# A hand-written order of 374 steps per two image pairs, exchanged for another order of the same steps

## The chip, the core and the metric

The kernel runs on one core of a Trainium2 chip. The metric is the device time of one execution in microseconds. Three runs of the kernel before gave 2715.25, 2713.97 and 2707.4 us, with a median of 2713.97 us. One further execution was profiled.

The engines are named as in the profile: PE is TensorE's matrix multiplier (PEld its weight loads), DVE is VectorE, ACT is ScalarE, POOL is GpSimd, and SP is the engine that issues every DMA of this kernel.

## The reference

The input is a batch of 128 images with 128 channels of 16 x 16 points. Layer 0 is a quantised convolution block. Layer 1 treats the 256 points of an image as a sequence of tokens, runs a selective state-space model (SSD, chunks of 64) over it forwards and backwards, and adds a mixture of 8 experts of which each token uses 2. Cut to what the change touches:

```python
t = _to_tokens(x)                                  # (128, 256, 128)
u = layernorm(t)
for dir in (fwd, bwd):                             # bwd sees the sequence reversed
    z, xbc, dt = split(u @ in_proj)
    xbc = silu(causal_conv(xbc, conv_w, 4 taps))   # -> xh (256), B (64), C (64)
    dt = softplus(dt + dt_bias)                    # exp, ln
    L = exp(segsum(dt * A))                        # exp, per head and chunk
    y = (C B^T * L) @ (xh * dt) + carried states + D * xh
    yg = y * silu(z)
    h += (yg * rsqrt(mean(yg * yg))) @ out_proj
t = t + h
p = softmax(layernorm(t) @ router_w); top 2, renormalised
out = t + sum over the 2 experts of p_e * (layernorm(t) @ expert_w[e])
```

## The kernel before

The program has two stages. The first (up to about 300 us) does the two convolutions and leaves each pair of images, transposed to tokens, in DRAM (`y_d`). The second stage is a loop over the 64 pairs, and the change is in its order alone.

The work of one pair is cut into generator functions, `part_a` to `part_t` (L691 to L1126). Each `yield` ends a step, and nearly every step puts the work of one engine into the program. `part_a` loads and normalises the tokens and transposes them (`u_ps`, L700). `part_c` is done once for two pairs: it makes the time steps `dt` and their logarithms, with one Exp (L738) and two Ln (L742 and L762) on ACT, and sends the parts through DRAM (`parts_d`) into the operands `rows` and `cols`. `part_x` projects one of three blocks of one direction (`x_ps`, L814), starts the convolution on ACT (L826) and finishes it by three DVE passes that read the bank in PSUM (L832). `part_bc`, `part_sx` and `part_z` apply Silu on ACT (L841, L851, L861). `part_s` makes the exponents of the decay matrix by a matmul (`sg`, L903 or L905) and applies Exp on ACT (L913). `part_g` makes C B^T (L888), `part_m` multiplies on DVE (L919, L924), `part_xt` transposes (L869), `part_y` multiplies (L938, L944), gates on DVE (L950) and POOL (L954) and squares on ACT (L957). `part_n` and `part_r` make the norm (L963, L971, L977, L979), `part_o` is the output projection (L998), `part_e` the router, `part_p` the product of gate and tokens on POOL (L1103), and `part_f` the experts (L1115). `part_t` has one step: it loads the table set of ACT that holds both Exp and Ln (L1125).

PSUM has three groups of banks in this stage, by `BANKS`: "x" with 2, "y" with 2 and "o" with 4. `x_ps`, `z_ps` and `sg` share the two "x" banks. A bank is free again when the last step that reads it is done: for `x_ps` the third DVE pass, for `z_ps` the Silu, for `sg` the Exp.

The order of all steps is written out by hand, in a table `T` (L1131 to L1196) with `PERIOD = 374`: for each step of an even and of an odd pair it gives a place, and pair `i` has its steps at `i // 2 * PERIOD` plus that place. The steps are sorted by this number and put into the program in that order, so that each engine's queue is in that order too:

```python
steps += [(i // 2 * PERIOD + t, len(steps) + n, stream) for n, t in enumerate(places[i % 2])]
steps.sort(key=lambda step: step[:2])
```

The number is a rank and not a time. Every two pairs bring 374 steps, so one period of the loop is 374 steps of several pairs in different stages, and a place says where in the period a step stands when it is taken modulo 374. There are 32 periods.

ACT holds one set of function tables at a time. Exp, Ln and Silu need a set that holds them. Where the set that is loaded lacks the next function, the program that is built has a table load ahead of that activation, under the activation's own line; in the profile it is `ACT_TABLE_LOAD`. The kernel's own load in `part_t` is one more.

Of the kernel before, what the change touches and what calls it, by code (L numbers as in the profile page):

```python
# [34 lines left out]
def kernel(ctx: ExitStack, tc: tile.TileContext, a: dict):  # L35
# [311 lines left out]
    with tc.tile_pool(name="w1p", bufs=1) as w1p:  # L347
# [15 lines left out]
        with tc.tile_pool(name="setup1", bufs=1) as setup, tc.tile_pool(  # L363
# [10 lines left out]
            for i in range(NP):  # L374
                t = res.tile([P, 2, NT], F32, name=f"xr{i}", tag=f"xr{i}")
# [38 lines left out]
            for c in range(4):  # L414
# [34 lines left out]
                n = cuts[c + 1] - cuts[c]  # L449
# [673 lines left out]
    def part_t(i):  # L1123
# [5 lines left out]

    PERIOD = 374  # L1130
    T = {  # L1131
        ('a',): [[145, 195, 294, 297, 323, 329], [338, 382, 482, 490, 514, 537]],
        ('c',): [
            [543, 573, 580, 590, 602, 607, 621, 627, 636, 638, 646, 647, 652, 657, 664, 666, 669, 696, 719,
             740, 765, 776, 790, 830, 835, 838, 929, 936, 968, 1102],
        ],
        ('x', 0, 0): [[735, 737, 748, 750, 753], [908, 920, 924, 926, 931]],
        ('x', 0, 2): [[755, 768, 769, 772, 775], [938, 946, 955, 957, 959]],
        ('x', 0, 1): [[786, 798, 804, 811, 814], [975, 982, 992, 1003, 1004]],
        ('x', 1, 2): [[821, 822, 832, 840, 846], [1022, 1034, 1039, 1041, 1049]],  # L1140
        ('x', 1, 0): [[839, 843, 853, 865, 866], [1044, 1056, 1057, 1059, 1061]],
        ('x', 1, 1): [[886, 894, 897, 900, 912], [1074, 1083, 1084, 1095, 1097]],
        ('z', 1, 0): [[898, 905], [1101, 1106]],
        ('bc',): [[928, 963], [1115, 1162]],
        ('sx', 0): [[901], [1098]],
        ('z', 0, 0): [[913, 925], [1116, 1118]],
        ('sx', 1): [[935], [1125]],
        ('z', 1, 1): [[934, 942], [1123, 1136]],
        ('z', 0, 1): [[945, 951], [1138, 1147]],
        ('g', 0): [[984], [1182]],  # L1150
        ('s', 0, 0, 0): [[958, 966], [1148, 1154]],
        ('t',): [[1344], [1203]],
        ('xt', 0, 0): [[993, 1006], [1169, 1180]],
        ('s', 0, 1, 0): [[969, 978], [1158, 1161]],
        ('s', 0, 0, 1): [[979, 987], [1168, 1173]],
        ('s', 0, 0, 2): [[989, 1000], [1183, 1184]],
        ('m', 0, 0): [[1011, 1016], [1200, 1201]],
        ('xt', 1, 0): [[974, 997], [1155, 1159]],
        ('s', 0, 1, 1): [[1007, 1014], [1190, 1194]],
        ('s', 1, 1, 0): [[1015, 1018], [1202, 1208]],  # L1160
        ('s', 0, 1, 2): [[1023, 1035], [1249, 1252]],
        ('xt', 0, 1): [[1008, 1032], [1163, 1192]],
        ('s', 1, 0, 2): [[1051, 1060], [1258, 1266]],
        ('g', 1): [[1069], [1248]],
        ('m', 0, 1): [[1078, 1080], [1256, 1259]],
        ('s', 1, 0, 0): [[1062, 1065], [1241, 1250]],
        ('s', 1, 1, 1): [[1082, 1091], [1232, 1234]],
        ('xt', 1, 1): [[1090, 1094], [1280, 1295]],
        ('s', 1, 0, 1): [[1064, 1066], [1251, 1254]],
        ('m', 1, 1): [[1110, 1120], [1261, 1264]],  # L1170
        ('s', 1, 1, 2): [[1073, 1075], [1235, 1242]],
        ('y', 0, 1): [[1099, 1105, 1113, 1134], [1276, 1290, 1296, 1322]],
        ('y', 0, 0): [[1096, 1100, 1104, 1126], [1265, 1277, 1281, 1315]],
        ('m', 1, 0): [[1081, 1107], [1292, 1293]],
        ('y', 1, 1): [[1121, 1128, 1176, 1181], [1297, 1307, 1347, 1351]],
        ('y', 1, 0): [[1144, 1174, 1179, 1187], [1324, 1341, 1364, 1370]],
        ('n', 0): [[1157], [1360]],
        ('n', 1): [[1199], [1376]],
        ('r',): [[1205, 1216, 1218, 1222, 1231], [1391, 1401, 1402, 1410, 1421]],
        ('o', 0): [[1233, 1247], [1404, 1426]],  # L1180
        ('o', 1): [[1219, 1246], [1424, 1441]],
        ('e',): [
            [1255, 1273, 1284, 1288, 1301, 1304, 1311, 1313, 1318, 1323, 1326, 1327, 1330, 1335, 1336, 1339,
             1354, 1357, 1368, 1372, 1373, 1383, 1387, 1393, 1398, 1399, 1403, 1407, 1411, 1420, 1453],
            [1442, 1459, 1462, 1482, 1486, 1491, 1506, 1511, 1514, 1515, 1519, 1525, 1527, 1539, 1540, 1541,
             1544, 1549, 1551, 1565, 1567, 1585, 1589, 1595, 1597, 1598, 1599, 1600, 1602, 1603, 1610],
        ],
        ('p', 0): [[1466, 1509, 1545], [1643, 1652, 1680]],
        ('p', 1): [[1463, 1493, 1571], [1644, 1719, 1720]],
        ('f',): [  # L1190
            [1505, 1530, 1560, 1563, 1572, 1581, 1617, 1627, 1631, 1637, 1736],
            [1663, 1688, 1708, 1733, 1753, 1802, 1806, 1811, 1824, 1835, 1881],
        ],
        ('p', 2): [[1477, 1526, 1611], [1657, 1739, 1801]],
        ('p', 3): [[1584, 1618, 1619], [1796, 1803, 1820]],
    }  # L1196
    parts = {
        "a": part_a, "c": part_c, "x": part_x, "bc": part_bc, "sx": part_sx, "z": part_z, "xt": part_xt, "g": part_g,
# [45 lines left out]
```

## Time and profile before

| what | value |
|---|---|
| runs | 2707.4, 2713.97, 2715.25 us |
| profiled execution: time | 2710.16 us |
| profiled execution: span from first to last instruction | 2708.4 us |
| busy share of the span | PE 93%, DVE 89%, ACT 79%, POOL 61% |
| granted TensorE clock, mean | 0.984 |
| time from one start of L778 to the next in the loop | 72.47 to 72.49 us from the fourth period on |
| ACT table loads in the profile | L913 66, L851 64, L1125 64; 1283 ns each |

The span is 1.8 us shorter than the execution's own time. The loop's `r_ps` matmuls (L774, L778), which come once in a period, run from 326 us to 2551 us. The period repeats to within 0.02 us, so one period of it stands for all but the first three and the last.

### The profile page before, as it was taken

The numbers are of one execution on the slowest core, as the hardware profiler recorded it, in microseconds if no ns is written. First come the engines' busy times: TensorE is split into PE (matmuls) and PEld (weight loads), VectorE is DVE, ScalarE is ACT, GpSimd is POOL, SyncE is SP. The second block draws the span as 40 slices with busy tenths as digits, with TensorE's granted clock in tenths as the row PEclk, the third lists the DMA queues.
The fourth block names the chain that finished last, engine by engine and source line by source line (L and its number), as shares of the span: only waits on it lengthen the run. The fifth ranks groups of instructions, "written<-read, shape, count | busy, mean of one in ns | idle before, by whom it ended". The sixth has DMA issues, their size and how long they took to land.

```text
span 2708.4 us, 47861 instructions
## 1 busy us (share of the span) xinstructions
PE 2528.8 (93%) x16004; PEld 1486.2 (55%) x16004; DVE 2405.0 (89%) x6161; ACT 2129.3 (79%) x3750; POOL 1656.0 (61%) x1728
## 2 busy tenths in 40 slices
PE   0889589999999999999999999999999999999997
PEld 0335245565565555566555565555555566555553
DVE  8876579999999999999999999999999999999884
ACT  6877488888888888888888888888888888888872
POOL 1885315666666666666666666666666666666566
PEclk9999789999999999999999999999999999999998
DMA  8468211223322233322322223222223322322223
GB/s 273 157 219 273 102 29 57 92 88 96 95 92 83 76 95 96 95 88 87 96 82 79 92 89 94 96 92 89 72 93 95 96 88 89 93 88 76 85 84 110
DMA packets 165707, 275.59 MB, mean 102 GB/s; under 512 B 46528, under 2 KB 89536, under 8 KB 165440
## 3 DMA queue, kind: packets, MB, share of 16 engines
q1 hardware_dynamic: 165440, 272.32, 32.0%
q8 instruction: 132, 2.16, 0.3%
q14 instruction: 135, 1.11, 0.1%
HBM read 197.45 MB, written 58.03 MB: 94 GB/s over the span
## 4 chain that ended last, share of the span: by engine, by line
PE 69%; DVE 16%; ACT 7%; DMA 3%; issue 3%; POOL 1%; SPq 0%; POOLq 0%; DVEq 0%; ACTq 0%
PE f_ps L1115 11%; PE x_ps L814 9%; PE o_ps L998 8%; PE y_ps L938 8%; PE z_ps L857 7%; PE cv L221 4%; PE y_ps L944 4%; PE sg L903 3%; PE g_ps L888 3%; PE xt_ps L869 2%; DVE bc L832 2%; ACT e L913 2%; DVE xc L832 2%; PE sg L905 2%; DMA xr<-in_x 2%
## 5 line engine op out<-in xcount | busy, mean ns | idle before, releaser
L1103 POOL TENSOR_TENSOR gb<-gb,u2T 128x512 f32<-128x512 f32 x512 | 643.3, 1278 | 48.8 <-DMA gb<-gd 44.3
L832 DVE SCALAR_TENSOR_TENSOR xc<-x_ps,cw,xc 128x510 f32<-128x510 f32 (+2 forms) x768 | 571.3, 744 | 76.4 <-ACT xc L826 58.7
L913 ACT ACTIVATE e<-sg 128x512 f32<-128x512 f32 x768 | 449.4, 594 | 213.2 <-PE sg L903 172.5
L954 POOL TENSOR_TENSOR yg<-yg,z 128x512 f32<-128x512 f32 x256 | 326.0, 1279 | 432.7 <-DVE yg L950 430.7
L1115 PE MATMUL f_ps<-gb,ew 128*128 128x512 f32 x1024 | 519.0, 606 | 7.1 <-POOL gb L1103 6.9
L814 PE MATMUL x_ps<-uT,wx 128*128 128x512 f32 x768 | 406.5, 611 | 15.6 <-ACT e L913 5.8
L938 PE MATMUL y_ps<-e,xt 128*64 128x256 f32 x2048 | 319.3, 390 | 0.6 <-DVE e L919 0.6
L919 DVE TENSOR_TENSOR e<-e,g_ps 128x1024 f32<-128x1024 f32 x256 | 310.4, 1212 | 1.9 <-PE g_ps L888 1.9
L832 DVE SCALAR_TENSOR_TENSOR bc<-x_ps,cw,bc 128x510 f32<-128x510 f32 (+2 forms) x384 | 284.3, 740 | 10.6 <-ACT bc L826 8.1
L857 PE MATMUL z_ps<-uT,wz 128*128 128x512 f32 x512 | 275.8, 621 | 0.2
L998 PEld LDWEIGHTS o_ps<-wo,yg 128*128 128x128 f32 x2048 | 246.1, 193 | 25.3 <-issue 16.7
L998 PE MATMUL o_ps<-wo,yg 128*128 128x128 f32 x2048 | 251.5, 276 | 0.0
L826 ACT ACTIVATE xc<-x_ps,cb,cw 128x512 f32<-128x512 f32 x256 | 199.2, 778 | 63.0 <-PE x_ps L814 62.7
L1115 PEld LDWEIGHTS f_ps<-gb,ew 128*128 128x128 f32 x1024 | 171.1, 192 | 115.6 <-issue 93.7
L950 DVE SCALAR_TENSOR_TENSOR yg<-xc,dcol,y_ps 128x512 f32<-128x512 f32 x256 | 187.3, 742 | 53.0 <-PE y_ps L944 53.0
L963 POOL TENSOR_TENSOR sq<-sq,sq 128x512 f32<-128x512 f32 x128 | 163.1, 1274 | 113.5 <-ACT sq L957 113.5
L944 PE MATMUL y_ps<-e,xt 128*64 128x128 f32 x2048 | 198.9, 273 | 0.0
L903 PE MATMUL sg<-rows,cols 128*128 128x256 bf16 x1024 | 191.9, 274 | 7.5 <-DVE bc L832 2.3
L221 PE MATMUL cv<-hpad,wq 128*128 128x512 bf16 x640 | 179.4, 424 | 16.4 <-DVE hpad L194 8.6
L944 PEld LDWEIGHTS y_ps<-e,xt 128*64 128x64 f32 x2048 | 147.0, 137 | 74.1 <-DVE e L924 0.3
L861 ACT ACTIVATE z<-z_ps 128x512 f32<-128x512 f32 x256 | 152.3, 595 | 40.2 <-PE z_ps L857 38.4
L903 PEld LDWEIGHTS <-cols 128*128 128x128 bf16 x1024 | 91.8, 100 | 156.7 <-issue 143.8
(258 smaller groups left out, 5010.1 us busy)
## 6 DMA issues: line engine op xcount, KB each, us to landing
gb<-gd SPq DMA_DIRECT2D x256, 512.0 KB
xr<-in_x SPq DMA_DIRECT2D x64, 256.0 KB
y<-yt SPq DMA_DIRECT2D x64, 256.0 KB
yt<-y SPq DMA_DIRECT2D x64, 256.0 KB
cc<-bc SPq DMA_DIRECT2D x128, 128.0 KB
out<-ob SPq DMA_DIRECT2D x64, 256.0 KB
o<-o SPq DMA_DIRECT2D x59, 256.0 KB
q<-o SPq DMA_DIRECT2D x59, 256.0 KB
```

The source lines that it names most:

```text
L814: nc.tensor.matmul(ps, wx[d][:, n * P : (n + 1) * P], uTs[i], start=True, stop=True)
L832: nc.vector.scalar_tensor_tensor(acc[:, :, to], raw[:, :, of], cw[:, d, n, 3 - back : 4 - back], acc[:, :, to], ALU.mult, ALU.add,)
L857: nc.tensor.matmul(ps, wz[:, d, n * P : (n + 1) * P], uTs[i], start=True, stop=True)
L903: nc.tensor.matmul(sg[:, :, of], c_[:, k, d, s, half, :], r_[:, :, d, t, of], start=True, stop=True)
L913: nc.scalar.activation(e0[:, :, t, :] if j < 2 else e1, sg, AF.Exp)
L919: nc.vector.tensor_tensor(e0.rearrange("p h t l -> p h (t l)"), e0.rearrange("p h t l -> p h (t l)"), gps[i, d, k][:, 0:NT].unsqueeze(1).t ...
L938: nc.tensor.matmul(y_ps[64 * q : 64 * q + 64, k, :], xt[:, 2 * k + s0, 64 * h : 64 * h + 64], e0[:, h].rearrange("p t l -> p (t l)"), star ...
L944: nc.tensor.matmul(y_ps[64 * q : 64 * q + 64, k, s1 * P : (s1 + 1) * P], xt[:, 2 * k + s1, 64 * h : 64 * h + 64], e1[:, h, :], start=False ...
L954: nc.gpsimd.tensor_tensor(yg, yg, zs[i, d][:, n, :], ALU.mult)
L998: nc.tensor.matmul(o_ps[:, (2 * j + d) * P : (2 * j + d + 1) * P], ygs[i, d, n][:, t * P : (t + 1) * P], wo[d][:, n, :], start=(n == 0), s ...
L1103: nc.gpsimd.tensor_tensor(gb[:, e], gb[:, e], u2Ts[i], ALU.mult)
L1115: nc.tensor.matmul(f_ps, ew[:, e, :], gbs[i, e], start=False, stop=(e == NE - 1))
```

## The change

The diff changes only the places in `T`. All 374 steps of a period, their instructions, tiles and buffers, `PERIOD` and the numbers of banks stay. Its author describes it as the same steps in a fourth order, searched with measured waits between engines and with half a microsecond kept between DVE's passes over SBUF and POOL's products. The pipeline is as deep as it was: from the first `x` step of an even pair to the last `f` step of the odd one there are 1146 ranks in both tables (735 to 1881 before, 665 to 1811 after).

The lines of the diff that the text below speaks of:

```diff
-        ('c',): [
-            [543, 573, 580, 590, 602, 607, 621, 627, 636, 638, 646, 647, 652, 657, 664, 666, 669, 696, 719,
-             740, 765, 776, 790, 830, 835, 838, 929, 936, 968, 1102],
+        ('c',): [
+            [484, 494, 507, 518, 531, 552, 560, 573, 576, 579, 600, 606, 613, 620, 649, 651, 652, 659, 661,
+             671, 691, 698, 709, 726, 730, 756, 778, 789, 891, 1002],
...
-        ('x', 1, 2): [[821, 822, 832, 840, 846], [1022, 1034, 1039, 1041, 1049]],
-        ('x', 1, 0): [[839, 843, 853, 865, 866], [1044, 1056, 1057, 1059, 1061]],
+        ('x', 1, 2): [[754, 759, 768, 780, 792], [938, 949, 952, 956, 963]],
+        ('x', 1, 0): [[775, 779, 794, 796, 801], [964, 973, 978, 983, 986]],
...
-        ('t',): [[1344], [1203]],
-        ('xt', 0, 0): [[993, 1006], [1169, 1180]],
-        ('s', 0, 0, 1): [[979, 987], [1168, 1173]],
-        ('s', 0, 0, 2): [[989, 1000], [1183, 1184]],
+        ('t',): [[591], [1118]],
+        ('xt', 0, 0): [[914, 922], [1087, 1120]],
+        ('s', 0, 0, 1): [[913, 918], [1098, 1108]],
+        ('s', 0, 0, 2): [[921, 927], [1109, 1127]],
...
-        ('s', 0, 1, 1): [[1007, 1014], [1190, 1194]],
-        ('s', 1, 1, 0): [[1015, 1018], [1202, 1208]],
-        ('xt', 0, 1): [[1008, 1032], [1163, 1192]],
+        ('s', 0, 1, 1): [[937, 945], [1123, 1132]],
+        ('s', 1, 1, 0): [[946, 957], [1139, 1147]],
+        ('xt', 0, 1): [[940, 962], [1093, 1131]],
...
-        ('y', 0, 0): [[1096, 1100, 1104, 1126], [1265, 1277, 1281, 1315]],
-        ('y', 1, 1): [[1121, 1128, 1176, 1181], [1297, 1307, 1347, 1351]],
-        ('y', 1, 0): [[1144, 1174, 1179, 1187], [1324, 1341, 1364, 1370]],
-        ('r',): [[1205, 1216, 1218, 1222, 1231], [1391, 1401, 1402, 1410, 1421]],
+        ('y', 0, 0): [[1029, 1034, 1037, 1111], [1213, 1218, 1226, 1275]],
+        ('y', 1, 1): [[1057, 1069, 1113, 1119], [1239, 1247, 1260, 1299]],
+        ('y', 1, 0): [[1075, 1103, 1114, 1124], [1257, 1284, 1303, 1306]],
+        ('r',): [[1140, 1151, 1155, 1158, 1164], [1328, 1341, 1343, 1345, 1356]],
...
-            [1663, 1688, 1708, 1733, 1753, 1802, 1806, 1811, 1824, 1835, 1881],
+            [1622, 1645, 1668, 1672, 1676, 1696, 1716, 1743, 1763, 1766, 1811],
```

The order of a step's numbers is the order of its yields. In `c` the sixth is the Exp (L738), the eighth the first Ln (L742) and the eighteenth the second (L762). In `x` they are the matmul, ACT's start of the convolution and the three DVE passes; in `s` the matmul and the Exp; in `r` the matmul (`n_ps`, L971), ACT's copy (L977), the transpose (L979) and two small steps.

## The prediction

> **What bounds the kernel now.** I read the busy shares first, then the table of one period, then who waited for whom, then the timelines of PE and ACT at those waits.
>
> ```profile
> PE 2528.8 (93%) x16004; PEld 1486.2 (55%) x16004; DVE 2405.0 (89%) x6161; ACT 2129.3 (79%) x3750; POOL 1656.0 (61%) x1728
> 1174.70:1247.20 72.50, 71.61 (x474) 43.12 (x473) 67.65 (x176) 59.54 (x105) 46.13 (x46) 1.00 0.28 89
> ```
>
> The second line is one period (us: length, then busy PE, PEld, DVE, ACT, POOL, then clock). PE has 0.9 us of idle in 72.5, DVE 4.8, ACT 13.0. The period is set by PE's queue: its matmuls plus its waits. Busy time hides part of a wait, since a matmul's end is modelled, so I took PE from start to start. A 128x512 fp32 product (x, z, f; two passes) takes 0.86 us, a 128x512 `sg` 0.22, four transposes 0.44, `o` 1.79, `y` 1.45, `g` 0.86, `n` 0.57. All 103 groups of a period follow such fixed values, except three, which wait: 0.90, 0.26 and 0.24 us, together 1.39. The largest, ACT's timeline and then PE's:
>
> ```profile
> 1145.77 1.28 ACT L913 ACT_TABLE_LOAD   x1
> 1147.08 0.60 ACT L913 ACTIVATE e<-sg 128x512 f32<-128x512 f32 x1
> 1147.70 1.28 ACT L1125 ACT_TABLE_LOAD   x1
> 1148.99 0.63 ACT L957 ACTIVATE sq<-yg 128x512 f32<-128x512 f32 x1
> 1149.53 0.58 ACT L913 ACTIVATE e<-sg 128x512 f32<-128x512 f32 x1
> ...
> 1148.40 1.02 PE L814 MATMUL x_ps<-uT,wx 128*128 128x512 f32 x2
> 1150.16 0.38 PE L905 MATMUL sg<-rows,cols 128*128 128x512 bf16 x1 [0.73 <-ACT e L913]
> ```
>
> The `sg` at 1150.16 could have started 0.86 us after 1148.40. It needs the "x" bank that the Exp ending at 1150.11 reads, and this Exp stands behind two table loads and a square. The 0.24 us wait is of the same kind:
>
> ```profile
> 1191.34 1.28 ACT L1125 ACT_TABLE_LOAD   x1
> 1192.64 0.60 ACT L913 ACTIVATE e<-sg 128x512 f32<-128x512 f32 x1
> ...
> 1192.09 1.12 PE L1115 MATMUL f_ps<-gb,ew 128*128 128x512 f32 x2
> 1193.29 1.12 PE L814 MATMUL x_ps<-uT,wx 128*128 128x512 f32 x2
> ```
>
> The third, 0.26 us at 1184.21, waits for the last DVE pass of an `x_ps`, late because a small product before it (`sel`, L1055, otherwise 0.19 us) took 1.13 us beside one of POOL's. So table loads on ACT, not ACT's sum, make most of PE's wait, because only two banks lie between them and PE.
>
> **The change, part by part.**
>
> *What stays.* Every instruction of PE, DVE, POOL and SP, and the depth of the pipeline. Fill and drain I leave at nothing: their ranks are nearly the same. 31 periods carry the change.
>
> *PE's own work.* After a full 128x128 product, a run that uses part of the array (`y`, `g`, `n`, `dt`, `rt`) starts 0.094 us later, and a full product behind it costs 0.01 (`sg`), 0.06 (transposes) or 0.10 us (128x512) more: above, `f` and `x` have 1.12 where they otherwise have 1.02. There are 13 such runs in a period before and 15 after: 2 x 0.094 = 0.19; behind them 0.92 becomes 0.95; a pair of `y` that stood together is split, 0.15. Sum **+0.37 us**.
>
> *DVE beside POOL.* DVE's rows above their usual time (`sel` L1055 and L1058, `e` L1071, up to 1.28 for 0.15) come to about 4.3 us a period. Spacing can take these away. They are 4.3 us of DVE's time, but PE's path holds only the 0.26.
>
> *The removed waits.* I count all three as gone: **-1.39**. That is the most the change can gain on PE's path.
>
> *Table loads.* This is what a change of order brings with it. Before, modulo 374, `t` of the even pair stands at 222, ahead of the Exp (233) and the two Ln (253, 322) of `c`: its set serves all three. After, Exp is at 178, the first Ln at 199, `t` only at 217. The built program's ACT order shows the result: 32 loads at the first Ln (2 before) and 95 at L913 (66 before); the Silu phases still have 64. Per period 8 loads, not 6: 2 x 1.28 = 2.57 us of ACT, against 13.0 idle. What counts is where they stand. ACT after: Exp(0,1,1), **load**, Ln, x(1,2), **load**, Exp(1,1,0), xt, **load** (`t`), ns. PE: sg(0,1,1), x(1,2), xt, sg(1,1,0), f, n, x(1,0), f, nT. x(1,0) takes the bank that Exp(1,1,0) frees. These are the rows for ACT:
>
> ```profile
> L913 ACT ACTIVATE e<-sg 128x512 f32<-128x512 f32 x768 | 449.4, 594 | 213.2 <-PE sg L903 172.5
> L826 ACT ACTIVATE xc<-x_ps,cb,cw 128x512 f32<-128x512 f32 x256 | 199.2, 778 | 63.0 <-PE x_ps L814 62.7
> L742 ACT ACTIVATE lw<-w 128x64 f32<-128x64 f32 x32 | 8.0, 249 | 0.0
> L913 ACT ACT_TABLE_LOAD x66 | 84.7, 1283 | 1.2
> ```
>
> From the start of sg(0,1,1): matmul and hand-over 0.42, Exp 0.59, load 1.28, Ln 0.25, x 0.78, load 1.28, Exp 0.59, hand-over 0.1: x(1,0) at 5.3. PE has 0.22 + 0.86 + 0.44 + 0.22 + 0.95 + 0.57 = 3.26 us of work until then: **2.0 us of wait**. Without the two loads the sum is 2.7 and there is none. The first load can't run earlier: it is queued behind an Exp that waits for this very matmul. Then nT needs ns: Exp's end at 5.25 + xt 0.58 + load 1.28 + ns 0.27 + 0.05 = 7.4; PE is there at 5.3 + 0.96 + 0.86 = 7.1: 0.3 more. If ACT comes late to Exp(0,1,1) (squares, an xt and `c`'s Exp stand ahead), up to 0.8 is added. I take **2.7**, ends 2.0 and 3.1.
>
> *The odd pair's `t`* stands at 370, between Exp(0,0,1) and Exp(0,0,2) with three squares and an xt. From the first Exp's end: 3 x 0.63 + 1.28 + 0.58 + 0.59 = 4.4 us until x(1,2) gets its bank; PE has sg 0.31, g 0.86, f 0.96, sg 0.22 = 2.35, and more if it reaches sg(0,0,2) late, which its two f (1.7 us) suggest. Ends 0 and 2.0; **1.2**. The nearest row, the load at 1191.34, cost 0.24. The loads at the turns to Silu and from Silu to Exp stand beside `y`, `u2` and `z` work of over 2 us; I cost them at nothing, and at 1.28 each if ACT is behind there.
>
> *Clock.* A long wait can also slow what follows. At the loop's start the trace has:
>
> ```profile
> 398.70 1.98 PE L814 MATMUL x_ps<-uT,wx 128*128 128x512 f32 x2 [1.85 <-ACT e L913]
> 400.69 2.69 PE L998 MATMUL o_ps<-wo,yg 128*128 128x128 f32 x16
> ...
> 398.80:402.20 3.40, 3.40 (x11) 2.26 (x12) 1.25 (x3) 0.80 (x2) 1.01 (x1) 0.50 0.28 63
> ```
>
> After 1.85 us of idle the granted clock was 0.50 for 3.4 us, a loss of 1.7; after 1.30 us (at 427) it stayed at 1.00. A wait of 2.0 to 2.7 in each period may or may not do this; I take half of 1.7, **0.85**, ends 0 and 1.7.
>
> *The sum.* 0.37 - 1.39 + 2.7 + 1.2 + 0.85 = **+3.73 us** a period, x 31 = 116 us. On the profiled execution (2710.2; span 2708.4) that is 2826; the median of the runs lies 3.8 higher, so 2830.
>
> **Two rules weighed.** The Trainium skill, "ScalarE: Activation LUTs", section on what a table load costs, adds a drain to each load, 2.66 us per switch. Here the load at 1145.77 takes 1.28 and the Exp follows 0.03 later; by the page's figure the two loads would make the wait 2.8 us longer, an estimate of 85 us more in all. The row decides. The Trainium skill, "TensorE: Matmul & The Clock Gate", Part 1, has the clock fall after an idle window of about 3.4 us, so a wait of 2.7 would leave it alone and the sum would be 26 us less. The row at 398.70 shows a fall after 1.85 us of idle, so the half stays in.
>
> **The rivals.**
> *Faster: the loads hide.* With no wait on PE left, the period falls by 1.02: 31 x 1.02 = 32 us, 2682. For it: 13.0 us of ACT idle per period, and 4.3 us that DVE can win back. It decides once Exp(1,1,0) ends within 3.2 us of sg(0,1,1)'s start. Against it: matmul, two Exp, Ln, x and two loads in one queue are 5.2.
> *Only the sure part.* Waits of 2.0 and nothing else: +0.98 a period, 30 us, 2744.
> *Worse.* Both places at their ends and the clock falling at both: 3.1 + 2.0 + 3.4 - 1.02 = 7.5, 231 us, 2945; half-way to it from my sum is 2887.
> *The spacing isn't there.* Delayed squares and Exps shift POOL and DVE against each other, and DVE's stalls return; PE, waiting elsewhere, then loses 0.26 more at most, 8 us.
> *No change:* the loads cost about the 1.0 that the rest gains.
>
> **How the numbers follow.** My sum 0.62, only the sure part 0.16, worse 0.12, faster 0.07, no change 0.03. The range goes from just under the sure part, 2740, to 2895, a little over half-way to the worst; outside lie the faster and unchanged cases and part of the worse one. A measurement of this kernel tells about 0.3% (8 us) from no change: faster 0.07, same 0.03, slower 0.90.
>
> **What would show it.** Right: table loads of 1.28 us at L742, about 255 loads at L742, L861, L913 and L1125 together; PE's longest waits at x_ps after an Exp (L913), 2 us or more, once a period; r_ps starts some 76 us apart; ACT busier by 2.6 us a period. The clock step shows as 0.5 in some stretches inside the loop. Wrong: periods of 71.5 us, or PE waits that end at DVE or POOL, or fill and drain that grow.

## The result and the profile after

The changed kernel takes 2792.11 us (median of 4 runs, 2786.04 to 2795.79), the kernel before 2712.38 us (4 runs). The ratio is 1.0294, with a 95% interval from 1.0269 to 1.0318: slower by 80 us.

All of it lies in the loop. In the profiled executions it was 2223.6 us from the first of the 32 starts of L778 to the last, and is 2304.9 us, 81.4 more; what lies ahead of them is 1.1 us longer and what follows 1.2 us shorter. The page's first part, and the table of two neighbouring periods of the loop and of one stretch inside the second (us: length, busy PE, PEld, DVE, ACT, POOL, then the granted clock):

```profile
PE 2561.8 (92%) x16004; PEld 1496.3 (54%) x16004; DVE 2386.0 (86%) x6161; ACT 2205.4 (79%) x3808; POOL 1658.5 (59%) x1728
1207.80:1282.30 74.50, 72.12 (x473) 43.16 (x473) 66.96 (x176) 62.23 (x107) 46.21 (x45) 1.00 0.29 87
1282.30:1358.20 75.90, 73.60 (x473) 44.07 (x473) 67.08 (x176) 62.16 (x107) 46.19 (x45) 0.98 0.27 86
1338.10:1341.50 3.40, 3.40 (x8) 1.62 (x7) 0.89 (x6) 2.24 (x4) 0.08 (x1) 0.53 0.00 0
```

There are two kinds of period now: 74.50 us, and 75.9 us where the granted clock falls to half for 3.4 us. In 27 settled periods there are 12 of the second kind. ACT has 2.7 us more to do in a period than before (62.2 for 59.5), with 58 more instructions in the whole program. All of them are table loads (the groups of ACT, by line):

```profile
L913 ACT ACT_TABLE_LOAD x95 | 121.9, 1283 | 1.7
L1125 ACT ACT_TABLE_LOAD x64 | 82.1, 1283 | 1.1
L861 ACT ACT_TABLE_LOAD x64 | 82.1, 1283 | 1.1
L742 ACT ACT_TABLE_LOAD x32 | 41.1, 1283 | 0.6
```

This is where PE waits. ACT's timeline of the stretch with the first Ln, and PE's below it:

```profile
1258.40 0.60 ACT L913 ACTIVATE e<-sg 128x512 f32<-128x512 f32 x1 [0.21 <-PE sg L905]
1259.01 1.28 ACT L742 ACT_TABLE_LOAD   x1
1260.31 0.26 ACT L742 ACTIVATE lw<-w 128x64 f32<-128x64 f32 x1
1260.47 0.76 ACT L826 ACTIVATE bc<-x_ps,cb,cw 128x512 f32<-128x512 f32 x1
1261.25 1.28 ACT L913 ACT_TABLE_LOAD   x1
1262.54 0.60 ACT L913 ACTIVATE e<-sg 128x512 f32<-128x512 f32 x1
1263.04 0.58 ACT L873 COPY xt<-xt_ps 128x512 f32<-128x512 f32 x1
1263.63 1.28 ACT L1125 ACT_TABLE_LOAD   x1
1264.93 0.28 ACT L977 ACTIVATE ns<-n_ps 128x128 f32<-128x128 f32 x1
...
1263.19 1.13 PE L814 MATMUL x_ps<-uT,wx 128*128 128x512 f32 x2 [1.88 <-ACT e L913]
1264.15 1.02 PE L1115 MATMUL f_ps<-gb,ew 128*128 128x512 f32 x2
1265.26 0.33 PE L979 MATMUL n_ps<-ident,ns 128*128 128x128 f32 x1
```

The Exp that starts at 1262.54 frees the bank for the `x_ps` at 1263.19, and the copy at 1264.93 makes the `ns` that the transpose at 1265.26 reads. Three loads stand in six microseconds, in the order that the prediction has. The 1.88 us in the bracket are idle time. From start to start, as the prediction reckons, the wait of `x_ps` is 1.95 us: the `n_ps` ahead of it starts at 1260.67 and takes 0.57. The transpose waits 0.24 us, since the `f_ps` ahead of it takes 0.86.

Where the clock falls, the same place looks like this one period later:

```profile
1337.69 1.53 PE L814 MATMUL x_ps<-uT,wx 128*128 128x512 f32 x2 [1.88 <-ACT e L913]
1339.01 1.91 PE L1115 MATMUL f_ps<-gb,ew 128*128 128x512 f32 x2
```

The wait is the same 1.88 us, but `x_ps` takes 1.53 for 1.13 and `f_ps` 1.91 for 1.02.

### The profile page after: what moved, and what is told of

Its sections match the earlier page's. It is cut to its first block, busy times and chain, and to the rows that moved or that the text cites. A ratio compares the mean times of both kernels' runs of the same rounds, so it can differ in the third digit from the quotient of the medians.

```text
span 2789.7 us, 47812 instructions
## 1 busy us (share of the span) xinstructions
PE 2561.8 (92%) x16004; PEld 1496.3 (54%) x16004; DVE 2386.0 (86%) x6161; ACT 2205.4 (79%) x3808; POOL 1658.5 (59%) x1728
## 4 chain that ended last, share of the span: by engine, by line
PE 76%; ACT 15%; DVE 5%; issue 1%; DMA 1%; POOL 1%; SPq 0%; DVEq 0%; POOLq 0%; ACTq 0%
PE f_ps L1115 12%; PE x_ps L814 11%; PE y_ps L938 9%; PE z_ps L857 8%; PE o_ps L998 8%; PE cv L221 4%; PE sg L903 4%; PE y_ps L944 4%; PE xt_ps L869 3%; PE g_ps L888 3%; ACT e L913 3%; ACT L1125 2%; ACT sq L957 2%; PE sg L905 2%; ACT L913 2%
## 5 line engine op out<-in xcount | busy, mean ns | idle before, releaser
L1115 PE MATMUL f_ps<-gb,ew 128*128 128x512 f32 x1024 | 532.8, 614 | 8.0 <-POOL gb L1103 7.7
L814 PE MATMUL x_ps<-uT,wx 128*128 128x512 f32 x768 | 417.8, 627 | 75.5 <-ACT e L913 68.4
L986 POOL TENSOR_TENSOR rr<-rr,mhalf 128x8 f32<-128x8 f32 x64 | 106.6, 1666 | 175.9 <-DVE rr L982 175.9
L814 PEld LDWEIGHTS x_ps<-uT,wx 128*128 128x128 f32 x768 | 125.0, 194 | 135.0 <-ACT e L913 86.3
```

Of the source, the lines that this page charges most:

```text
L814: nc.tensor.matmul(ps, wx[d][:, n * P : (n + 1) * P], uTs[i], start=True, stop=True)
L1115: nc.tensor.matmul(f_ps, ew[:, e, :], gbs[i, e], start=False, stop=(e == NE - 1))
```

## The experiments

Theory L says that the table loads make PE's waits, by where they stand between two Exps. Rival O says that the rest of the new order makes them and that the loads fit into ACT's idle time. As `t` (L1125) is a step of its own that no other step waits for, it can be moved alone. A place with a half is a rank between two others. Each ratio is to runs of the kernel before on the same chip. The periods are from start to start of L778 in each run's trace.

**e1: the order after, `t` ahead of the first Exp of each pair.**

```diff
-        ('t',): [[591], [1118]],
+        ('t',): [[888.5], [1084.5]],
```

> The order after, with only the step t moved: ahead of the first Exp (L913) of each pair, at 888.5 and 1084.5. 4 table loads a period instead of 8. Theory L (the table loads make TensorE's waits): the waits of 1.95 us (x_ps behind an Exp), 0.24 (transpose of ns) and 0.39 us (x_ps of the odd pair) go, the granted clock stays at 1.00 in the loop, the period falls from a mean of 75.07 us to 71.5 to 71.9, and the time to about 2689 us (2683 to 2695), below both kernels. Rival O (the rest of the order makes the waits, and the loads fit into ScalarE's idle time): at least 2760 us.

Measured: 2681.95 us, ratio to before 0.9891 (0.9874 to 0.9907). The period is 71.77 to 71.80 us, and the granted clock stays at 1.00 through the settled loop. PE's wait for the Exp and the wait for `ns` are gone; so is the wait of `x_ps` in the odd pair. The wait of 0.37 us behind a DVE pass stays and is 0.39. Only the place of `t` differs from the changed kernel, and 110 us are gone. That settles L against O. (The time lies 1 us below the range that was expected.)

**e2: the order before, with the same move.**

```diff
-        ('t',): [[1344], [1203]],
+        ('t',): [[965.5], [1153.5]],
```

> The order before, with only the step t moved ahead of the first Exp (L913) of each pair, at 965.5 and 1153.5. 4 table loads a period instead of 6. Theory L: the waits of 0.90 and 0.24 us go, the 0.26 us behind a DVE pass stays; period 72.48 - 1.14 = 71.34 us, time about 2677 us. Rival O: 2712 us as before, within 5.

Measured: 2665.43 us, ratio 0.9831 (0.9815 to 0.9848), period 71.18 us. Two of the three waits of before are gone and the third is left. One line makes the kernel before faster by 1.7%. The period of e1 lies 0.6 us above it: 0.24 us is PE's own work, and the rest is waits, 0.15 more behind the DVE pass and 0.22 at `r_ps` (L774). So with the loads well placed in both, the new order is still the slower one, by 17 us.

**e3: the order after, only the even pair's `t` moved.**

```diff
-        ('t',): [[591], [1118]],
+        ('t',): [[888.5], [1118]],
```

> The order after, with only the even pair's t moved, to 888.5; the odd one stays at 1118. 5 loads a period, none left in the stretch with the first Ln. Theory L: the waits of 1.95 and 0.24 us and the half clock go, those of the odd pair (0.39 and 0.37) stay: period 72.3 us, time about 2706 us. Rival O: within 10 us of 2792.

Measured: 2696.34 us, ratio 0.9946 (0.9930 to 0.9963), period 72.24 to 72.26 us (expected 72.3), clock at 1.00. The waits of 0.39 and 0.37 us of the odd pair are as they were. The periods of e1 to e3 came within 0.2 us of what was expected, but the times came out 7 to 12 us lower. Part of that lies in the first three periods, in which the loop fills: they take 186.9, 185.7 and 190.2 us together, for 194.6 before the change and 202.9 after it.

**e4: the order after, only the odd pair's `t` moved.**

```diff
-        ('t',): [[591], [1118]],
+        ('t',): [[591], [1084.5]],
```

> The order after, with only the odd pair's t moved, to 1084.5; the even one stays at 591. 7 loads a period; the three loads in the stretch with the first Ln stay. Theory L: TensorE's wait of 0.39 us (x_ps of the odd pair, behind the load at t) goes, that of 0.37 us (sg behind a DVE pass) stays, and the waits of 1.95 and 0.24 us and the half clock stay: about 13 us less than 2792, 2780 (2765 to 2790). Rival: the odd pair's t matters as much as the even one's, half of the 110 us between e1 and the order after: 2737.

Measured: 2784.14 us, ratio 1.0283 (1.0266 to 1.0300). The wait of 0.39 us is gone and the periods without a half clock fall from 74.50 to 74.04 us, as L has it. But 20 of 27 periods now have the half clock (75.4 us), for 12 before, and that gives most of the gain back: 8 x 1.38 / 27 = 0.41 us a period for 0.46 won. The mean of the settled periods is 75.06 us, for 75.12 in the changed kernel, and most of the 8 us of difference in time lies in the first three periods (195.5 us for 202.9). The rival's 2737 is far off.

**e5: the order before, made to load as the order after does.**

```diff
-        ('t',): [[1344], [1203]],
+        ('t',): [[1400.5], [1203]],
```

> The order before, with only the even pair's t moved to 1400.5, behind the first Ln and two more Exps, as it stands in the order after. 8 loads a period; the stretch becomes Exp, load, Ln, xt, load, Exp, Exp, load, ns. Theory L: x_ps waits about 2.4 us and the transpose of ns about 1.0 us there, the wait of 0.90 us goes; 2.5 us more a period, and a half clock in part of the periods; about 2800 us (2770 to 2833). Rival O: 2712 us, within 10.

Measured: 2785.63 us, ratio 1.0279 (1.0262 to 1.0297), most periods 75.15 to 75.36 us. Moving one load costs the old order nearly all of what the whole change cost. ACT's stretch and PE's:

```profile
1326.13 1.28 ACT L742 ACT_TABLE_LOAD   x1
1327.43 0.26 ACT L742 ACTIVATE lw<-w 128x64 f32<-128x64 f32 x1
1327.59 0.57 ACT L873 COPY xt<-xt_ps 128x512 f32<-128x512 f32 x1
1328.18 1.28 ACT L913 ACT_TABLE_LOAD   x1
1329.47 1.08 ACT L913 ACTIVATE e<-sg 128x512 f32<-128x512 f32 x2
...
1328.30 0.64 PE L971 MATMUL n_ps<-sq,chosen 128*32 128x128 f32 x16 [0.65 <-POOL rstda L681]
1330.12 1.96 PE L814 MATMUL x_ps<-uT,wx 128*128 128x512 f32 x2 [1.18 <-ACT e L913]
```

Part of the wait I had put at `x_ps` shows at `n_ps` ahead of it (0.7 us from start to start; `x_ps` 1.2), 2.0 in all for the 2.4 expected. The transpose of `ns` waits 0.9 us in a period without a half clock, for the 1.0 expected. The profile's releaser for `n_ps` names POOL's `rstda`, which no matmul there reads; what `n_ps` waited for was not settled. The wait of 0.90 us behind the old place of the even `t` is gone.

**e6: the order after, the even pair's `t` directly ahead of the first Ln.**

```diff
-        ('t',): [[591], [1118]],
+        ('t',): [[572.5], [1118]],
```

> The order after, with the even pair's t moved to 572.5, directly ahead of the first Ln: 6 loads a period, as before the change, and one load instead of three between the Exp of sg(0,1,1) and ns. Theory L: the wait of x_ps falls by one load, from 1.95 to about 0.67 us, that of the transpose of ns goes, and with an idle time below 1 us the granted clock stays at 1.00: period 72.9 us, time about 2724 us (2710 to 2740). Rival (the number of loads counts, not their place): the kernel before has 6 loads too, so 2712.

Measured: 2715.6 us (7 runs), ratio 1.0029 (1.0017 to 1.0040), period 72.78 us (expected 72.9), clock at 1.00. One load in the stretch leaves a wait of 0.53 us at `x_ps`. With none (e3) it is 0, with two and a third for `ns` it is 1.95 and 0.24. The time alone lies between the two theories' numbers and nearer the rival's 2712; the traces tell them apart, since the waits that stay are 0.53, 0.39 and 0.37, other ones than the 0.90, 0.26 and 0.24 of before.

**e7 and e8: two costs that are left in e2, one each.** In e7 the odd pair's `y(0,1)` matmul stands directly behind `y(0,0)`, one run of part-array products fewer. In e8 the odd pair's first `sel` (L1055) stands behind the last DVE pass of `x(0,2)`.

```diff
 e7 (on e2), ('y', 0, 1), odd pair
-[1276, 1290, 1296, 1322]
+[1265.5, 1290, 1296, 1322]
 e8 (on e2), ('e',), odd pair
-[1442, 1459, 1462, 1482, 1486, 1491, 1506, 1511, 1514, 1515, 1519, 1525,
+[1442, 1459, 1462, 1482, 1486, 1491, 1506, 1511, 1514, 1515, 1523.5, 1525,
```

> The kernel of e2, with one PE step moved: the odd pair's y(0,1) matmul from 1276 to 1265.5, directly behind y(0,0) and ahead of z(1,0), so that one run of part-array products fewer stands in the period (12 for 13). If a run costs what the rows of before show (0.094 ahead of it, 0.15 for the split pair, 0.06 behind), the period falls by 0.30 us to 70.88 and the time by 9 us to about 2656. If y(0,1) then waits for DVE's products instead: 71.18 us, 2665, with the wait at y_ps.

> The kernel of e2, with one DVE step moved: the odd pair's first sel (L1055) from 1519 to 1523.5, behind the last DVE pass of x(0,2) instead of between its passes. This sel takes 1.13 us instead of 0.19 when it starts beside a product of POOL, and TensorE's last wait (0.24 us, sg) is for that last pass. Theory: the wait goes, the period falls to 70.94 us and the time by 7 us to about 2658. Rival (the stall moves to another step that TensorE waits for): 71.18 us or more, 2665.

Measured: e7 2654.65 us, ratio 0.9805 (0.9787 to 0.9823), period 70.88 us; e8 2656.48 us, ratio 0.9808 (0.9792 to 0.9825), period 70.95 us. Both periods are what the rows gave (70.88 and 70.94). DVE's timeline at the place, first of e2, then of e8:

```profile
1233.52 0.74 DVE L832 SCALAR_TENSOR_TENSOR bc<-x_ps,cw,bc 128x510 f32<-128x510 f32 x1
1234.17 1.13 DVE L1055 TENSOR_TENSOR sel<-lg,mx 128x32 f32<-128x32 f32 x1
1235.23 1.51 DVE L832 SCALAR_TENSOR_TENSOR bc<-x_ps,cw,bc 128x508 f32<-128x508 f32 x2
```

```profile
1226.35 2.30 DVE L832 SCALAR_TENSOR_TENSOR bc<-x_ps,cw,bc 128x510 f32<-128x510 f32 x3
1228.57 0.18 DVE L1055 TENSOR_TENSOR sel<-lg,mx 128x32 f32<-128x32 f32 x1
```

The three passes are now in one piece, and `sel` takes 0.18 us for 1.13.

**e9: e2, e7 and e8 together.**

> The kernel of e2 with the moves of e7 (y pair) and e8 (sel) together. Theory: the two gains add, since one is TensorE's own work and the other its last wait: period 71.18 - 0.30 - 0.24 = 70.64 us, time about 2647 us. Rival (without waits TensorE now catches up with ScalarE or VectorE, and a new wait takes their place): 2652 to 2657, no better than e7 or e8 alone.

Measured: 2649.69 us, ratio 0.9776 (0.9760 to 0.9792), period 70.64 us. It is the fastest version, 1.2% below e1 and 5.1% below the changed kernel. The theory's sum holds for the period to 0.01 us. PE has no wait of over 0.1 us left in the period: the 70.64 us are its matmuls.

## Why the prediction was right, point by point

The direction, the mechanism and the place were right, and the time lay inside the range (2740 to 2895), 38 us below the 2830 that was forecast. The sum per period was +3.73 us. Measured, a period without a half clock is 74.50 - 72.48 = 2.02 us longer, and 12 half clocks in 27 periods at 1.4 add 0.62: 2.64, times 31 is 82 us. Most terms were put too high.

*PE's own work, forecast +0.37.* Without the waits and the small delays that go with them the periods of the two orders are 71.18 and 70.94 us: +0.24. The price of a run of part-array products is right (e7, exact to 0.01 us); counting the rows of two orders by hand left an error of 0.13. One row was misread: the prediction explains the 1.12 us of the `x_ps` at 1193.29 by such a run, but a full product (`f_ps`) stands ahead of it. It has its extra 0.10 us behind the wait, and in e2, without the wait, that is gone.

*The removed waits, -1.39.* All three are gone, as counted; with that 0.10 us, and 0.06 us at an `xt_ps` that is gone in e2 too, they were 1.54.

*The stretch with Ln, forecast 2.7.* Measured 1.95 at `x_ps` and 0.24 at the transpose, 2.2. The chain from sg(0,1,1) to x(1,0) was put at 5.3 us and takes 5.2 (1257.98 to 1263.19). What failed is the allowance on top of the minimum of 2.0 + 0.3: ACT was not late at the first Exp. The bracket in its row says so, it waited 0.21 us for PE.

*The odd pair's `t`, forecast 1.2.* This term was too large: x(1,2) waits 0.39 us. ACT, PE and DVE at the place:

```profile
1294.09 1.28 ACT L1125 ACT_TABLE_LOAD   x1
1295.38 0.63 ACT L957 ACTIVATE sq<-yg 128x512 f32<-128x512 f32 x1
1295.92 0.57 ACT L873 COPY xt<-xt_ps 128x512 f32<-128x512 f32 x1
...
1296.95 0.39 PE L905 MATMUL sg<-rows,cols 128*128 128x512 bf16 x1 [0.21 <-DVE xc L832]
1297.55 1.13 PE L814 MATMUL x_ps<-uT,wx 128*128 128x512 f32 x2 [0.21 <-ACT e L913]
...
1294.31 1.15 DVE L1055 TENSOR_TENSOR sel<-lg,mx 128x32 f32<-128x32 f32 x1
```

Two things were missed. Neighbouring activations overlap by about 0.1 us (the copy starts at 1295.92, the square ends at 1296.01), so the chain is 4.0 us and not 4.4. And PE comes to it later, because it waits 0.37 us just before, at `sg`, for a DVE pass; with it the place costs 0.8.

*DVE beside POOL.* The change is described as keeping DVE's passes over SBUF away from POOL's products. The stalls did not go away, they moved: in each period three rows of DVE are 0.7 to 1.1 us above their usual time, all beside a product of POOL (L1055 twice and L1065), 2.8 us together; before there were four (L678, L1055, L1058, L1071), 3.4 us. DVE's busy time in a period falls from 67.65 to 66.96. One of the three, the `sel` at 1294.31 above, takes 1.15 us between the passes of the `x_ps` whose bank `sg` waits for. In the old order e8 took the same pattern out, and the wait went. That move was not tried in the new order, so for its 0.37 us the cause is read from the rows and not shown.

*A wait that no term had.* PE starts `r_ps` (L774) 0.11 us late and runs it 0.11 us longer, 0.21 a period in all; the profile names a DVE product (L924) as what it waits for.

*The clock, forecast 0.85 as half of 1.7.* The clock falls in 12 of 27 periods, 0.44, and costs 1.4 each: 0.62. A wait of 1.88 us can be enough, as the row at 398.70 of before had shown. The Trainium skill ("TensorE: Matmul & The Clock Gate", Part 1) speaks of an idle window of about 3.4 us. That half of the periods was nearly right is luck: in e4 the same wait, with a period 0.46 us shorter, had the half clock in 20 of 27.

*The drain.* The Trainium skill ("ScalarE: Activation LUTs", "What ACT_TABLE_LOAD costs") adds a drain of 1.38 us to each load. It does not show on either side of a load in the stretch: the Exp ends 0.01 us ahead of the load at 1259.01, and the Ln starts 0.02 us after the load's end. In the trace of before, 195 of the 196 loads behind 330 us have the next activation within 0.03 us.

*The rivals.* "The loads hide" was priced at 2682, and the order after takes 2682 once the loads stand elsewhere (e1). That the two figures agree so closely is partly chance: the period of e1 is 71.8 us where that price has 71.5, and the shorter first periods make up for it. "The spacing isn't there" came true in one place, and at 0.37 us cost a little more than the 0.26 that it was given.

*The signs.* The loads are 255, as named, and ACT is busier by 2.7 us for 2.6. The longest wait is where it was put, at 1.95 us just under the 2 that was named, and the periods average 75.1 us for "some 76". One sign of being wrong showed as well, a wait that ends at DVE (0.37 us); it is a small part of the 3.3 us of waits and what goes with them.

## What to carry to other kernels

When an order of steps is changed by hand or by a search, look at what is put in between the steps by the build: here table loads, most of which no step of the table names, cost 110 us by their number and place (the changed kernel against e1), and all else that the change moved 17 us (e1 against e2). Where two banks lie between two engines, the cost of a load is read from the chain between the two matmuls that share a bank, and not from the idle time of its engine: 13 us of idle a period did not hide 2.6 us. A step that loads a set for several functions belongs ahead of the first activation of the phase that needs any of them, where the build would insert a load anyway. In e2 that is the first Exp behind the Silus: 4 loads a period for 6, and no wait of PE at them. In e6, on the new order, the step stood directly ahead of the first Ln, and 6 loads and a wait of 0.53 us were left.

## What the runs showed of the hardware

The granted clock fell for stretches of 3.41 us, or of whole multiples of it, and the starts of these stretches lie on one fixed grid of 3.41 us (in the changed kernel's trace successive ones in the settled loop are 150.19 or 225.28 us apart, 44 and 66 times 3.413). Whether the same wait in the same place meets a half clock goes by where it ends on this grid. In the changed kernel `x_ps` waits 1.88 us in each settled period. The clock fell in the 12 in which the wait ended 0.02 to 0.60 us ahead of a point of the grid, and stayed in the 15 in which it ended at such a point or up to 0.8 us behind it. In e4 it fell in 20 of 27, at 0.05 to 1.06 us ahead. Two waits of 0.7 and 1.2 us close together brought it in 24 of 27 periods of e5. Single waits of up to 0.9 us in a period (before, e6) never did in the settled loop. Where the limit lies in between was not measured.

I had not expected what this does to the mean period. In the changed kernel a period with a half clock is 75.89 us, 0.80 longer than 22 stretches of the grid (75.09), and the next wait ends later on the grid; one without is 74.50, 0.59 shorter, and the next wait ends earlier. The settled periods of the changed kernel, e4 and e5 average 75.12, 75.06 and 75.12 us, though their periods without a half clock are 74.50, 74.04 and 74.44. So the 0.46 us that e4 won at PE's waits came back as more half clocks.
